# Fused filter, code and mixture-of-experts kernel: whole tiles counted in two parts, means and scales in the lists' entries

## Chip, cores and metric

The kernel runs on one core of one Trainium2 chip, in one launch. The metric is device time in microseconds: the median of the runs of a kernel, each the time of that one core. Three runs of the kernel before gave 1426.52 us at the median, 1426.07 to 1428.13.

## The reference

The input x is 16 x 1024 tokens of 512 numbers (16,384 tokens, fp32). For each token:

```python
xn = layernorm(x)                                   # no weights
x1 = ifft(fft(xn) * filt).real                      # filt from the first 1024 numbers of xn
bits = sigmoid(x1 @ W_el + b_el) > 0.5              # 24 bits
corrected = golay_correct(bits)                     # syndrome of 12, up to 3 flips
s = x1 + corrected @ W_le + b_le
probs = softmax(xn @ router_w.T)                    # 8 experts
top 2 of probs; weights = top2 / (sum + 1e-6)
ffn = sum over the two: (xn @ expert_w[e] + prob[e]) * weight[e]
out = x + s * silu(ffn)
```

So each token needs two products of 512 x 512 with the weights of its own two experts.

## The kernel before

Tokens are worked on 128 at a time, a *tile*; there are 128 tiles. The kernel has two passes.

**Pass 1** (`pass_1`, a loop over token tiles g) runs over the tokens in their order. Per tile: sums on VectorE (`total`) and squares on ScalarE (`spread`) for mean and scale; folding of the input into its even and odd halves (`fold`, one part of it, `mm`, on GpSimd); four transposes and the filter matmuls on TensorE (`transpose`, `filt`), whose output also holds the 24 code values and the 8 router values; evacuation on ScalarE, and a store of the filtered part to the DRAM tensor `yd` per four tiles (`store`, SyncE's queue). Per eight tiles the code is corrected (`code`: bits, two turns by TensorE, syndrome, correction). Per *round* of tiles the router runs (`route`): some fifty small VectorE steps that find the two largest experts, their weights and the position of each token in a list, and then one scatter DMA per tile (`scatter`, GpSimd's queue) that writes the token's number to that position in the DRAM tensor `lists`. There are 28 lists, one for each pair of experts. Rounds have 16 tiles up to tile 96, then 8, and at last 4 and 4. The steps of a round wait in the Python list `routes`; `push(n)` emits up to n of them per tile (4, then 7, then three times 12) and stops at a `None`, and `throw` emits one or two scatters per tile. All emission is by hand (`manual_schedule`): each engine executes its instructions in the order in which the program emits them, and a wait holds all that follows on that engine. `put_records` stores 32 numbers per token (weights, bias, mean in column 10, scale in column 11, code bits) to the first columns of `yd`.

After the last tile the last round runs alone, then the counts: `whole_a`, `whole_b` and `whole_c` work out how many full tiles of 128 each pair's list holds, fetch the list rows of the 101 *whole tiles* by one indirect DMA (`tt`, L887) and transpose them, which gives `toks` (the token of each partition for each whole tile) and `woff` (the two experts of each whole tile). `rest_a`, `rest_b`, `rest_c` work out where the remaining tokens of each list lie (`row_r`).

**Pass 2** runs over 189 tiles in an order fixed in advance: 101 *whole* tiles (one pair of experts for all 128 tokens, two products of four 512-wide steps each, L1186), 61 *items* (rest tokens gathered for one expert, one product, result stored to `ed`), and 27 *rests* (rest tokens again, which gather their two results from `ed` as `part0` and `part1`). The order is 10 wholes, then 61 items with 18 wholes among them, 4 wholes, then 27 rests with 69 wholes among them, each rest ahead of two or three wholes. The loop's turn n emits, in this order, work for tiles ahead and behind:

```python
each(n + AHEAD_K, fetch_tok)      # 9 ahead: list entries of items and rests
each(n + AHEAD_X, fetch_x)        # 6 ahead: x, and the row of yd
each(n + AHEAD_P, fetch_parts)    # 4 ahead: rests only
each(n + AHEAD_N, normalize)      # 3 ahead: DVE
each(n + AHEAD_N + 1, triple)     # 4 ahead: copy of the code bits, DVE
each(n, spread_out); each(n - 1, combine)          # DVE
put(tiles[n - 4])                 # BEHIND = 3: out <- xg, indirect DMA
work_on(tiles[n], beside)         # products; beside: turn(n+2), mend(n+1), turn_code(n+3)
```

All gathers and `put` are indirect DMAs on GpSimd's queue. `gather` is the helper at L1108; the write-out to `out` is L1266. `combine` adds into the buffer of x (`xg`) and `put` writes it out, so this buffer is held from `fetch_x` until its write-out has landed. Buffers per name: `xg` 14, `yg` (the row of `yd`) 11, `xn2` 4, `res` 3. The pools of pass 1 are closed before pass 2; the framework makes an instruction wait for the last user of a buffer that it takes over. Address work of items and rests (`side`) runs one step per turn on VectorE.

Of the kernel before, what the change touches and what calls it, by code (L numbers as in the profile page):

```python
# [22 lines left out]
BITS = 24  # L23
# [9 lines left out]
def kernel(  # L33
# [31 lines left out]

    nc = tc.nc
# [20 lines left out]
    NITEM = 2 * NREST + NE - 1  # L87

# [4 lines left out]
    lists = dram.tile([NPAIR * N, 1], I32, name="lists")  # L93
# [8 lines left out]

    p1 = ExitStack()

    front = p1.enter_context(tc.tile_pool(name="front", bufs=2))
    xin = p1.enter_context(tc.tile_pool(name="xin", bufs=5))
    work = p1.enter_context(tc.tile_pool(name="work", bufs=2))
    sp = p1.enter_context(tc.tile_pool(name="sp", bufs=1))
    small = p1.enter_context(tc.tile_pool(name="small", bufs=3))
    mid = p1.enter_context(tc.tile_pool(name="mid", bufs=1))  # L110
    p1c = p1.enter_context(tc.tile_pool(name="p1c", bufs=1))
    cs = p1c.tile([P, X + Q], F32, name="cs")
    cd = p1c.tile([P, X + Q], F32, name="cd")
    cm = p1c.tile([P, 2, X + H], F32, name="cm")
# [10 lines left out]
    NR = 6 * NPAIR + 2 * NPAIR  # L125
    ord_sb = p1c.tile([NPAIR, orders.shape[1]], F32, name="ord_sb")
    upto_o = ord_sb[:, 0:NPAIR]
    uptoid_o = ord_sb[:, 0 : 2 * NPAIR]
    at = 2 * NPAIR
# [48 lines left out]
    zero = w_sb[:, NE - 4, 0, :].bitcast(I32)  # L178
# [55 lines left out]

    def clear_lists():
        nc.gpsimd.memset(zero, 0)
        nl = NPAIR * N // P // 512
        nc.gpsimd.dma_start(
            out=lists.rearrange("(p a n) o -> p a (n o)", p=P, a=nl),
            in_=zero.unsqueeze(1).to_broadcast([P, nl, 512]),  # L240
        )
# [170 lines left out]

    PAIRED = NT - 4 * GT
    rounds = [(t, 2 * GT) for t in range(0, PAIRED, 2 * GT)]
    rounds += [(t, GT) for t in range(PAIRED, NT - GT, GT)]
    rounds += [(NT - GT, TPT), (NT - TPT, TPT)]
# [3 lines left out]
    ps_g = p1.enter_context(tc.tile_pool(name="ps_g", bufs=2, space=PSUM))  # L420
# [3 lines left out]
    recs = [p1c.tile([P, 2 * GT, META], F32, name=f"rec{i}") for i in range(3)]  # L424
# [13 lines left out]
    for s in range(NG):  # L438
        groups[s].rec = recs[(s // 2) % 3][:, (s % 2) * GT : (s % 2 + 1) * GT, :]
# [28 lines left out]
    def spread(g: int):  # L468

        k, j = groups[g // GT], g % GT  # L470
        no = small.tile([P, E], BF16, name="no", bufs=2)
        nc.scalar.activation(  # L472
            no, xts[g // TPT][:, g % TPT, :], AF.Square, bias=k.sum[:, j : j + 1],
            scale=-float(E), accum_out=k.sq2[:, j : j + 1],
        )
# [81 lines left out]
    def take_ex(b: int, first: int = 0, past: int = TPT):  # L557

        s, a = b * TPT // GT, b * TPT % GT
        k = groups[s]  # L560
        if s * GT < PAIRED and s % 2:
            k.ex = groups[s - 1].wide[:, GT:]
        elif a + first == 0:
            k.wide = front.tile([P, 2 * GT, X], F32, name="ex")
            k.ex = k.wide[:, 0:GT]
        y = ybs[b][:, first:past]
        nc.vector.tensor_add(k.ex[:, a + first : a + past], y[:, :, 0, 0:X], y[:, :, 1, 0:X])
# [55 lines left out]
    def put_records(t, n):  # L623
        r = recs[(t // (2 * GT)) % 3]
# [6 lines left out]
    def route(n: int):  # L631
# [17 lines left out]
        def begin():  # L649
            s, j = t0 // GT, t0 % GT  # L650
            st.ex = (groups[s].wide if t0 < PAIRED else groups[s].ex)[:, j : j + S]
            st.rec = recs[(t0 // (2 * GT)) % 3][:, t0 % (2 * GT) : t0 % (2 * GT) + S, :]
            st.mx = st.m1 = new("mx", [P, S])
            v.tensor_reduce(st.mx, st.ex[:, :, L:X], AX.X, ALU.max)

# [36 lines left out]
        final = n + 1 == len(rounds)  # L692
        ops = [begin] if final else [begin, shift]
        ops += largest(lambda: st.ex[:, :, L:X], "hot1")
        if final:
            ops += [shift]
# [90 lines left out]
        def scatter(j):  # L787
# [4 lines left out]
                in_=tok[:, t0 + j : t0 + j + 1],  # L792
# [40 lines left out]
        if final:  # L833
            return ops + [None, rank, quads] + ranks + [None] + chances + weights
        ops += [quads, None, rank] + chances + weights
        ops += [lambda: put_records(t0, S)] if t0 + GT < NT else []
        return ops + ranks
# [9 lines left out]
    toks = bt.tile([P, NPURE], I32, name="toks")  # L847
    woff = bt.tile([1, 2 * P], I32, name="woff")
# [12 lines left out]
    def whole_a():  # L861

        pc = ps_g.tile([P, 512], F32, name="pg")[0:NPAIR, 0:P]
        nc.tensor.matmul(pc, cum, ones_b, start=True, stop=True)
        md.full = mid.tile([NPAIR, P], F32, name="full")
        floors(md.full, pc, 0.5 - P / 2)
        md.cnt = mid.tile([NPAIR, P], F32, name="cntk")
        nc.vector.tensor_copy(md.cnt, pc)

    def whole_b():  # L870

        po = ps_g.tile([P, 512], F32, name="pg")[:, 0 : 2 * NPAIR]
        nc.tensor.matmul(po, md.full, uptoid_o, start=True, stop=True)
        f = mid.tile([P, NPAIR], F32, name="upto_f")
        nc.vector.tensor_copy(f, po[:, 0:NPAIR])
        step = mid.tile([P, NPAIR], F32, name="step")
        nc.vector.tensor_scalar(step, po[:, NPAIR:], -1.0, float(NT), ALU.mult, ALU.add)
        scr = mid.tile([P, NPAIR], F32, name="scr")
        at = mid.tile([P, 3], F32, name="at3")
        for i, st_ in enumerate((step, steplo_r, stephi_r)):  # L880
            nc.vector.scalar_tensor_tensor(
                scr, f, tf, st_, ALU.is_le, ALU.mult, accum_out=at[:, i : i + 1]
            )
        idx = mid.tile([P, 1], I32, name="idx")
        nc.vector.tensor_add(idx, at[:, 0:1], tf)
        md.tt = mid.tile([P, P], I32, name="tt")
        nc.gpsimd.indirect_dma_start(  # L887
            out=md.tt[0:NPURE, :],
            out_offset=None,
            in_=lists.rearrange("(r c) o -> r (c o)", c=P),  # L890
            in_offset=bass.IndirectOffsetOnAxis(ap=idx[0:NPURE, :], axis=0),
            bounds_check=NPAIR * N // P - 1,
            oob_is_err=False,
        )
        pi = ps_g.tile([P, 512], F32, name="pg")[0:1, 0 : 2 * P]
        for h in range(2):
            nc.tensor.matmul(
                pi[:, h * P : (h + 1) * P], at[:, 1 + h : 2 + h], ident, start=True, stop=True
            )
        for h in range(2):  # L900
            nc.vector.tensor_scalar(
                woff[:, h * P : (h + 1) * P], pi[:, h * P : (h + 1) * P], float(h), None, ALU.add
            )

    def whole_c():

        tf_ = mid.tile([P, P], F32, name="ttf")
        nc.vector.tensor_copy(tf_[0:NPURE, :], md.tt[0:NPURE, :])
        pt = ps_g.tile([P, 512], F32, name="pg")[:, 0:NPURE]
        nc.tensor.transpose(pt, tf_[0:NPURE, :], ident[0:NPURE, 0:NPURE])  # L910
        nc.vector.tensor_copy(toks, pt)

    def rest_a():

        ph = ps_g.tile([P, 512], F32, name="pg")[0:NPAIR, 0:P]
        nc.tensor.matmul(ph, upto_o, md.full, start=True, stop=True)
        md.h = mid.tile([NPAIR, P], F32, name="h")
        nc.vector.tensor_scalar(md.h, ph, float(NPURE), None, ALU.min)

    def rest_b():  # L920

        pl = ps_g.tile([P, 512], F32, name="pg")[0:NE, 0:P]
        nc.tensor.matmul(pl, len_o[:, 0:NE], md.cnt, start=True, stop=False)
        nc.tensor.matmul(pl, len_o[:, NE:], md.h, start=False, stop=True)
        md.c = mid.tile([NE, P], F32, name="c")
        floors(md.c, pl, P / 2 - 0.5)

    def rest_c():
        pr = ps_g.tile([P, 512], F32, name="pg")[:, 0:NR]
# [4 lines left out]
        nc.vector.tensor_copy(row_r, pr)  # L934
# [4 lines left out]
    step_i = row_r[:, 4 * NPAIR + SEG :]  # L939
    GI = 8  # L940

    def item_adr(j: int, room):
# [6 lines left out]
            qf[:, j : j + n].unsqueeze(2).to_broadcast([P, n, SEG]),  # L949
# [5 lines left out]
        nc.vector.tensor_add(adr_i[:, j : j + n], jump, qf[:, j : j + n])  # L955

    def item_experts(room):
# [8 lines left out]
        with nc.allow_low_precision("whole numbers"):  # L966
            nc.vector.tensor_reduce(ioff[:, 0:NITEM], cmp, AX.X, ALU.add)

    def rest_adr(i: int, room, first, past):
# [14 lines left out]
        nc.vector.tensor_add(adr_r[:, i, first:past], jump, q)  # L984

    def pass_1():
        now, routes, scales = [], [], []

        def push(n):

            done = 0
            while routes and done < n:
                op = routes.pop(0)
                if op is None:
                    return
                op()
                done += 1

        def throw(n):
            for _ in range(min(n, len(scatters))):  # L1000
                scatters.pop(0)()
# [15 lines left out]
        for g in range(-2, NT):  # L1017
            if (g + AHEAD_L) % TPT == 0 and 4 <= (g + AHEAD_L) // TPT < NB:
                xts[(g + AHEAD_L) // TPT] = load_block((g + AHEAD_L) // TPT)
            if g == 2:  # L1020
                clear_lists()
# [4 lines left out]
            if g == NT - 1:  # L1026
                take_ex(NB - 1, 0, TPT - 1)
# [16 lines left out]
            if g % GT == 1 and g > 1:  # L1044
                now = code(g // GT - 1)
            if g == NT - TPT:
                last = code(NG - 1)
            for n, (t, size) in enumerate(rounds):
                if g == t + size + 1:
                    routes += route(n)  # L1050
            if now:
                now.pop(0)()
            if g < PAIRED:
                push(4)
            elif g < NT - TPT:
                push(7)
            else:
                for _ in range(3):
                    push(12)
# [389 lines left out]
```

## Time and profile before

| what | us |
|---|---|
| median of three runs | 1426.52 |
| the profiled execution, device time | 1425.39 |
| its span, first to last instruction | 1423.6 |
| last filter matmul of pass 1 starts | 355.86 |
| first expert product of pass 2 starts | 397.76 |
| last product of pass 2 ends | 1414.2 |
| expert products (L1186) busy on TensorE | 942.1 |
| GpSimd busy (917 instructions, mostly indirect DMAs) | 926.1 |
| VectorE busy / ScalarE busy | 955.1 / 594.2 |

The profile is one execution. "Busy" counts instructions with work; gaps are put down to what ended them, in the form `[idle <-releaser]`. "issue" means that nothing the profile shows was waited for. PE is TensorE's matmul, PEld its weight load, DVE is VectorE, ACT ScalarE, POOL GpSimd, SP SyncE. A line of the timeline has the start in us, the length in us, the engine, the line of the kernel, the operation and its operands. The landing time of a DMA runs from the start of the issuing instruction.

### The profile page before, as it was taken

Reading aid. Unit: us, or ns where it says so; the run is one execution under the profiler, and the core shown is the slowest. Engines: PE = TensorE matmul, PEld = TensorE weight load, DVE = VectorE, ACT = ScalarE, POOL = GpSimd, SP = SyncE. Lnnn points to the kernel's source line nnn. Section 1 sums busy time; section 2 is a strip of 40 time slices with the busy share of each in tenths; the row PEclk is TensorE's granted clock in tenths of the full one; section 3 lists DMA queues with packets and bytes.
Section 4 is the critical chain, followed back from the end, with each engine's and each line's share of the span. In section 5 each row is a group of like instructions: output and inputs, shape, how many; then the busy total and the mean of one; then the engine's idle time right before and its main releaser. Section 6 shows DMA issues by size and latency. Waiting matters only on the chain.

```text
span 1423.6 us, 18981 instructions
## 1 busy us (share of the span) xinstructions
PE 1349.6 (95%) x5189; PEld 760.1 (53%) x5189; DVE 955.1 (67%) x2703; ACT 594.2 (42%) x1297; POOL 926.1 (65%) x917
## 2 busy tenths in 40 slices
PE   2999999988399999999999999999999999999997
PEld 2888888766144444444444444444444444444443
DVE  7798888898368733333323336777877778777785
ACT  4889899875022222222222232333333333333332
POOL 1347777786464676676666567777777777777731
PEclk9999999999589999999999999999999999999999
DMA  5898777743141343444444465555555555555521
GB/s 202 320 322 279 225 230 238 215 130 98 55 136 63 129 147 108 137 138 114 122 145 127 123 190 171 174 169 171 165 175 172 173 173 166 173 173 160 182 95 45
DMA packets 119317, 232.39 MB, mean 163 GB/s; under 512 B 35925, under 2 KB 70565, under 8 KB 115118
## 3 DMA queue, kind: packets, MB, share of 16 engines
q0 software_dynamic: 49472, 135.96, 32.2%
q1 hardware_dynamic: 68638, 94.43, 20.4%
q8 instruction: 46, 0.75, 0.2%
q10 hardware_dynamic: 1104, 0.78, 0.2%
q14 instruction: 57, 0.47, 0.2%
HBM read 144.00 MB, written 87.10 MB: 162 GB/s over the span
## 4 chain that ended last, share of the span: by engine, by line
PE 65%; issue 5%; POOL 2%; DMA 1%; DVE 1%; POOLq 0%; ACT 0%; DVEq 0%
PE pe L1186 58%; PE pt L1159 5%; PE pe L1218 2%; POOL out L1266 1%; DMA tt<-lists,idx 0%; PE pc L1207 0%; POOL xg L1108 0%; POOL yg L1108 0%; DMA yg<-yd,toks 0%; DVE acc L1234 0%; DMA xg<-in_x,toks 0%; DVE yg L1223 0%; POOL part L1108 0%; POOL lists L789 0%; DVE mix L1260 0%
## 5 line engine op out<-in xcount | busy, mean ns | idle before, releaser
L1186 PE MATMUL pe<-w_sb,xt 128*128 x2104 | 942.1, 596 | 0.4 <-ACT ct L1211 0.4
L1186 PEld LDWEIGHTS pe<-w_sb,xt 128*128 128x128 f32 x2104 | 387.2, 190 | 425.4 <-issue 413.7
L1235 ACT ACTIVATE acc<-acc,yg 128x512 f32<-128x512 f32 x128 | 92.5, 722 | 407.5 <-DVE acc L1234 407.5
L1234 DVE SCALAR_TENSOR_TENSOR acc<-pe,yg,acc 128x512 f32<-128x512 f32 x101 | 75.7, 749 | 217.3 <-PE pe L1186 217.3
L1266 POOL DMA_INDIRECT out<-xg,toks x101 | 109.7, 1086 | 84.4 <-DVE xg L1261 63.7
L1161 ACT COPY xt<-pt 128x512 f32<-128x512 f32 x162 | 93.8, 579 | 163.7 <-PE pt L1159 112.5
L512 POOL TENSOR_TENSOR mm<-xt 128x256 f32<-128x256 f32 x128 | 98.6, 771 | 96.2 <-PE pt L519 70.9
L539 PE MATMUL py<-cm,pmt 128*128 128x288 f32 x512 | 158.9, 434 | 0.0
L789 POOL DMA_INDIRECT lists<-tok,dst x128 | 130.7, 1021 | 41.3 <-issue 20.7
L1108 POOL DMA_INDIRECT xg<-in_x,toks x101 | 108.9, 1078 | 39.7 <-issue 33.2
L1108 POOL DMA_INDIRECT yg<-yd,toks x101 | 106.3, 1053 | 33.3 <-issue 23.8
L1231 ACT ACTIVATE acc<-pe,yg 128x512 f32<-128x512 f32 x101 | 68.9, 682 | 139.9 <-PE pe L1186 119.4
L1159 PEld LDWEIGHTS pt<-ident,xn 128*128 128x128 f32 x648 | 81.5, 142 | 85.0 <-issue 84.1
L1223 DVE TENSOR_TENSOR yg<-pe,yg 128x512 f32<-128x512 f32 x128 | 87.3, 682 | 58.8 <-PE pe L1218 58.8
L1108 POOL DMA_INDIRECT rec<-yd,at x61 | 63.2, 1036 | 83.5 <-DVE at L1131 71.0
L542 ACT ACTIVATE yb<-py,rec 128x576 f32<-128x576 f32 x128 | 94.9, 741 | 39.9 <-PE py L539 39.2
L1108 POOL DMA_INDIRECT xg<-in_x,tok x88 | 93.8, 1066 | 26.9 <-issue 26.9
L1159 PE MATMUL pt<-ident,xn 128*128 128x128 f32 x648 | 98.2, 275 | 0.2
L539 PEld LDWEIGHTS py<-cm,pmt 128*128 128x128 f32 x512 | 89.1, 194 | 13.9
L472 ACT ACTIVATE no<-xt,sum 128x512 bf16<-128x512 f32 x128 | 91.0, 711 | 2.0 <-DVE pp L452 2.0
L1261 DVE TENSOR_TENSOR xg<-mix,xg 128x512 f32<-128x512 f32 x128 | 88.6, 692 | 4.4
L1260 DVE TENSOR_TENSOR mix<-mix,acc 128x512 f32<-128x512 f32 x128 | 87.9, 687 | 4.5 <-ACT acc L1235 4.5
(255 smaller groups left out, 1817.1 us busy)
## 6 DMA issues: line engine op xcount, KB each, us to landing
xt<-in_x SPq DMA_DIRECT2D x32, 1024.0 KB, 9.3
yd<-yb SPq DMA_DIRECT2D x64, 512.0 KB, 4.7
ed<-res SPq DMA_DIRECT2D x61, 256.0 KB, 3.5
w_sb<-in_expert_w SPq DMA_DIRECT2D x8, 1024.0 KB
yd<-rec SPq DMA_DIRECT2D x32, 64.0 KB, 2.9
lists<-tok,dst POOLq DMA_INDIRECT x128, 4.8
lists<-w_sb POOLq DMA_DIRECT2D x1, 1792.0 KB, 8.8
xg<-in_x,toks POOLq DMA_INDIRECT x101, 3.5
```

What stands on the lines that cost most here:

```text
L472: nc.scalar.activation(no, xts[g // TPT][:, g % TPT, :], AF.Square, bias=k.sum[:, j : j + 1], scale=-float(E), accum_out=k.sq2[:, j : j + 1],)
L512: nc.gpsimd.tensor_tensor(m, xr[:, 0:H], xr[:, H:E], ALU.subtract)
L539: nc.tensor.matmul(py[:, 1, 0 : X + H], pmt[:, 2 + c, :], cm[:, c, :], start=(c == 0), stop=(c == 1))
L542: nc.scalar.activation(y_room(g), py[:, :, 0:WY], AF.Copy, scale=k.rec[:, j, 11:12])
L789: dma = nc.gpsimd.indirect_dma_start(out=lists, out_offset=bass.IndirectOffsetOnAxis(ap=st.dst[:, j : j + 1], axis=0), in_=tok[:, t0 + j : ...
L1108: nc.gpsimd.indirect_dma_start(out=dst, out_offset=None, in_=src, in_offset=bass.IndirectOffsetOnAxis(ap=idx, axis=0), bounds_check=limit - 1,
L1159: nc.tensor.transpose(pt[:, c * P : (c + 1) * P], k.xn[:, c * P : (c + 1) * P], ident)
L1161: nc.scalar.copy(k.xt.rearrange("p c t -> p (c t)"), pt)
L1186: nc.tensor.matmul(pe.unsqueeze(1), k.xt[:, c, :], w_sb[:, bass.ds(e, 1), c, :], start=(c == 0), stop=(c == KC - 1),)
L1235: nc.scalar.activation(k.acc, k.acc, AF.Silu, bias=k.rec[:, 9:10])
L1261: nc.vector.tensor_add(k.x, k.mix, k.x)
L1266: dma = nc.gpsimd.indirect_dma_start(out=of, out_offset=bass.IndirectOffsetOnAxis(ap=k.tok, axis=0), in_=k.x, in_offset=None, bounds_check ...
```

## The change

- **Lists hold entries of three words**: mean, scale, token. The scatter sends columns 10 to 12 of the record (`ENTRY`), and `begin` of each round copies the tokens to column 12. The code bits move up in the record (`BITS` 24 to 26). Lists are no longer cleared at the start; `item_ends` caps item positions at the end of each expert's section (`qc`) instead.
- **Counting in two parts.** `whole_a`, `whole_b`, `whole_c` and `rest_a` become `whole_ops(part)`, a list of small steps in the queue `aside`. Part 0 takes 30 whole tiles from the lists as they stand after tile 80 and runs inside pass 1; its fetch waits until the scatters known at that point have been emitted. Part 1 takes the other 71 and runs in pass 2. `toks`, `woff` and the new `stats` (means and scales, turned along with the tokens) exist once per part.
- **All rounds have 16 tiles**, `push` takes 4 steps and `throw` one scatter per tile throughout pass 1. The last round, the code of the last eight tiles, part 1 of the counts, `rest_b` to `rest_e` and the address work run in `beside` of pass 2's turns, up to ten steps and three scatters a turn.
- **Order of pass 2**: 28 wholes, 61 items, 5 wholes, 27 rests with 68 wholes among them.
- **Gathers**: an item's or rest's list entry brings mean and scale, so items no longer gather a record (`rec`, with its VectorE step `at`). The row of `yd` is gathered by a step of its own, `fetch_y`, 4 tiles ahead instead of 6.
- **Buffers**: `xg` 11 (14), `yg` 7 (11), `xn2` 3 (4), `res` 2 (3), `recs` 4 (3). The pools `small`, `mid`, `p1c` and the PSUM pool `ps_g` stay open through pass 2; `turn_code` takes its PSUM from `ps_g`. `xin` is now the first pool of pass 1.

The diff, cut to its core:

```diff
+ENTRY = slice(10, 13)
-BITS = 24
+BITS = 26
...
+    SOON = 80
+    PARTS_OF = (30, NPURE - 30)
...
-    lists = dram.tile([NPAIR * N, 1], I32, name="lists")
+    lists = dram.tile([NPAIR * N, 3], I32, name="lists")
...
+    RT = 2 * GT
+    rounds = [(t, RT) for t in range(0, NT, RT)]
...
             v.tensor_reduce(st.mx, st.ex[:, :, L:X], AX.X, ALU.max)
+            v.tensor_copy(st.rec.bitcast(I32)[:, :, 12], tok[:, t0 : t0 + S])
...
-                in_=tok[:, t0 + j : t0 + j + 1],
+                in_=st.rec.bitcast(I32)[:, j, ENTRY],
...
+    def whole_ops(part: int):
...
+        def lengths():
+            nonlocal due
+            due = thrown[0] + len(scatters)
+            k.pc = ps_g.tile([P, 512], F32, name="pg")[0:NPAIR, 0:P]
+            nc.tensor.matmul(k.pc, cum, ones_b, start=True, stop=True)
...
+        def fetch():
+            if thrown[0] < due:
+                return False
+            nc.vector.tensor_copy(woff[part], k.pi)
+            k.tt = mid.tile([P, P, 3], I32, name="tt")
+            nc.gpsimd.indirect_dma_start(
+                out=k.tt[0:n].rearrange("t c o -> t (c o)"),
...
+        aside.extend([lengths, None, full, None, rows_, None, where, upto, None, experts])
+        aside.extend([bounded, None, fetch, None, None, apart, None, turned, None, kept])
...
-            if g == 2:
-                clear_lists()
+            if g == 20:
+
+                put_records(NT - RT, RT, recs[3])
...
                 if g == t + size + 1:
-                    routes += route(n)
+                    routes.extend(route(n))
+                    if t + size == SOON:
+                        routes.append(lambda: whole_ops(0))
...
+            push(routes, 4)
+            push(aside)
+            throw(1)
...
-    AHEAD_K, AHEAD_X, AHEAD_P, AHEAD_N, AHEAD_T = 9, 6, 4, 3, 2
+    AHEAD_K, AHEAD_X, AHEAD_P, AHEAD_Y, AHEAD_N, AHEAD_T = 9, 6, 4, 4, 3, 2
...
-    xgp = ctx.enter_context(tc.tile_pool(name="xgp", bufs=14))
+    xgp = ctx.enter_context(tc.tile_pool(name="xgp", bufs=11))
...
+    def fetch_y(k):
         if k.kind == "item":
...
-            row = w2.tile([P, E + META], F32, name="yg", bufs=11)
...
+            return
+        row = w2.tile([P, E + META], F32, name="yg", bufs=7)
+        gather(row, yd, k.tok, N)
...
-    LEAD, PAUSE, AMONG = 10, 4, 18
+    LEAD, PAUSE, AMONG = 28, 5, 0
...
+    now += code(NG - 1)
+    routes += route(len(rounds) - 1) + [lambda: whole_ops(1)] + [None] * 7
+    routes += [rest_b, None, rest_c, None, rest_d, None, rest_e, None]
...
                 each(n + AHEAD_N, turn_code)
+                if n < 0:
+                    return
+                if now:
+                    now.pop(0)()
+                push(routes, 10)
+                push(aside)
+                throw(3)
```

## Prediction

> **What bounds the kernel now.** I read the page's busy shares and slices first, then the seam between its two passes on TensorE, then that seam on GpSimd (POOL), then POOL late in pass 2.
>
> ```profile
> PE 1349.6 (95%) x5189; PEld 760.1 (53%) x5189; DVE 955.1 (67%) x2703; ACT 594.2 (42%) x1297; POOL 926.1 (65%) x917
> ...
> PE   2999999988399999999999999999999999999997
> ...
> POOL 1347777786464676676666567777777777777731
> PEclk9999999999589999999999999999999999999999
> ```
>
> TensorE is the bound, but for one hole in slices 8 to 10. The table by stretches measures it: TensorE has no gap in pass 2 and is mostly idle before.
>
> ```profile
> 348.00:392.00 44.00, 13.83 (x61) 9.03 (x61) 19.71 (x118) 3.88 (x9) 22.37 (x22) 0.55 0.17 47
> ...
> 398.00:1414.00 1016.00, 1016.00 (x2996) 489.63 (x2996) 629.69 (x1424) 308.18 (x602) 681.59 (x639) 1.00 0.48 146
> ```
>
> (Columns after the length: busy us of PE, PEld, DVE, ACT, POOL.) The hole's edges, and what POOL does in it:
>
> ```profile
> 355.86 2.27 PE L539 MATMUL py<-cm,pmt 128*128 128x288 f32 x4
> ...
> 397.76 5.06 PE L1186 MATMUL pe<-w_sb,xt 128*128 x8 [0.39 <-ACT ct L1211]
> ...
> 403.37 7.08 PE L1186 MATMUL pe<-w_sb,xt 128*128 x16
> ```
>
> ```profile
> 369.55 0.97 POOL L789 DMA_INDIRECT lists<-tok,dst  x1 [0.31 <-issue]
> 375.10 2.28 POOL L887 DMA_INDIRECT tt<-lists,idx  x1 [4.57 <-issue]
> 383.91 1.05 POOL L1108 DMA_INDIRECT xg<-in_x,toks  x1 [6.53 <-DVE toks L911]
> 387.67 1.00 POOL L1108 DMA_INDIRECT yg<-yd,toks  x1 [2.71 <-DVE row_r L934]
> ```
>
> The last filter matmul ends at 358.1; the first expert product starts at 397.8. Between them come scatters, their landing, the list fetch, and the first gathers. Last, POOL in the tail of pass 2, where whole tiles and rests alternate:
>
> ```profile
> 1023.60 1.09 POOL L1266 DMA_INDIRECT out<-xg,tok  x1 [0.30 <-DVE mix L1227]
> 1024.99 1.03 POOL L1108 DMA_INDIRECT xg<-in_x,tok  x1 [0.30 <-issue]
> 1026.33 1.01 POOL L1108 DMA_INDIRECT yg<-yd,tok  x1 [0.31 <-issue]
> 1027.65 1.03 POOL L1266 DMA_INDIRECT out<-xg,toks  x1 [0.30 <-issue]
> 1028.98 1.03 POOL L1108 DMA_INDIRECT tok<-lists,adr_r  x1 [0.30 <-issue]
> 1030.32 1.23 POOL L1108 DMA_INDIRECT xg<-in_x,toks  x1 [0.31 <-issue]
> ```
>
> It issues one indirect DMA after another. Its groups from 850 to 1250 us are 274 instructions, 295 us busy, 105 us idle; 274 gaps of 0.30 are 82 of these, so POOL really waits only some 22 us in 400. Busy share (74%) hides that it is **94% occupied**, one step behind TensorE. The page's landing times matter next:
>
> ```profile
> out<-xg,toks POOLq DMA_INDIRECT x101, 3.0
> ```
>
> **What the Trainium skill says.** "DMA: Bandwidth & Descriptors", section "Anatomy of one DMA — SWDGE (gpsimd) path": a semaphore wait is served on the issuing sequencer before dispatch, and each DMA has about 2.0 us of fixed cost, mostly the write receipt. The trace agrees: `out` lands 3.0 us after its start, 1.03 of them POOL's. "Perfetto Trace Analysis", section "Optimization Strategy": an equal bubble that repeats can mean that buffers ran out; before has none on TensorE. "TensorE: Matmul & The Clock Gate", section "What's actually happening": about 3.4 us idle halve the clock. The trace agrees: PEclk 5 in slice 10, and 5.06 us for eight products that later take 3.46.
>
> **The change, part by part.**
>
> *Pass 1.* Y evacuations on ScalarE stand at 39.98 (token tile 0), 264.60 (tile 96) and 358.16 (tile 127): 2.34 us a tile, then 3.02, when `push(7)` and rounds of 8 and 4 begin. Rounds of 16 at `push(4)` go on throughout, so I take 31 x 2.34: tile 127 at 337.1. The count behind tile 80 adds small matmuls, some 1.5 us of TensorE, and one fetch on POOL. That fetch stands behind the last scatter's landing (4.57 us of waiting in the trace) and takes 2.28; the next round's scatter, in the same step, may not write the lists before the fetch has landed (6.84 us from its start). Queued behind is `mm`, which the transposes need, at most two tiles (4.7 us) ahead. So TensorE loses 0 to 8 us; I take 5. Tile 127: 343.6. Clearing the lists (8.8 us of DMA near the start) goes: nothing, since TensorE stays at 100% over it. Entries of 12 bytes instead of 4 keep the instruction count and 128 elements; no row shows them: -5 to +5 us, value 0.
>
> *Start of pass 2.* Tokens, means and scales of 30 whole tiles are known; `xg` can be gathered early, but `yg` needs the last y store: 343.6 + 0.74 evacuation + 4.7 landing = 349.0. From the first `yg` to the first product took 397.76 - 387.67 = 10.1 us; the order of gathers is the same, so the product starts at 359.1: **38.7 us earlier**. The cold clock after the hole stays.
>
> *What moved into pass 2.* TensorE: code, rank and list matmuls of the hole sum to 10.0 us at the half clock, some 5.5 at full clock, plus 1.5 for a rank of 16 tiles: **+7**. VectorE: a whole tile costs 5.0 us (ten rows' means, from xn 0.54 to acc 0.75) of a 7.63 us turn; a round of 16 sums to 13.3 us over six turns, 2.2 each: 7.2, it fits. ScalarE: at most two more function-table switches; "ScalarE: Activation LUTs", section "What ACT_TABLE_LOAD costs", gives 1.28 us, no run here shows it; ScalarE is 30% busy: 0, without that cover 2.6. POOL: round 6 begins at step 113 and reaches its scatters ten steps of `push(4)` later, so 5 of its 16 go out in pass 1; 11 and round 7's 16 are left, three a turn; with xg, yg and out 6 x 1.34 = 8.0 us against 7.63; and scatters wait for `dst`, which VectorE makes in the same turn, with all gathers queued behind. The last records' store on SP waits for the `yg` gathers before it, and later ones wait for it (2.9 us). Count matmuls sit right behind `cum` in one turn (2 to 3 us of TensorE), and code turns share two PSUM buffers with the counts (2 + 1.5). With 3 for POOL I take **+10**, range 3 to 20. Items lose 61 `rec` gathers and `at` steps on POOL and DVE: 0, TensorE has no gap there now. The order (28 wholes, items, 5 wholes, rests) has the same products.
>
> So the seam gives -38.7 + 7 + 10 = **-22** (-32 to -5).
>
> *Buffers.* This decides. At the top of turn n a buffer for the x of tile n+6 is taken. Tiles n-4 to n+5 hold ten: tile n-4 is written out only at that turn's end. Of 14 buffers four are free, the oldest for four turns. **Of 11 one is free: that of tile n-5, whose `out` was POOL's last instruction of the turn before.** So each `xg` must wait until that `out` has landed. POOL is in order: `yg`, the parts and the next `out` are queued behind, VectorE's code copy and sum wait for that `yg` (its lead shrinks from 6 turns to 4, with 7 buffers for 11), and TensorE waits for both. Price: `xg` starts 3.0 + 0.25 after `out` starts, not 1.38 (1.08 + 0.30): **+1.87 us a turn**; with a `tok` gather between, 3.25 - 2.76 = +0.49. Items hold no buffer after normalizing, and early turns have slack (3 x 1.38 + 1.87 = 6.0 against 7.63). In the tail a cycle is one rest and 68/27 = 2.52 wholes. TensorE: 2.52 x 7.63 + 0.66 = 19.9. POOL: 6 + 7.56 = 13.56 gathers x 1.38 = 18.7, plus 2.52 x 1.87 + 0.49 = 5.2: **23.9 us**. POOL becomes the bound by 4.0 us a cycle. Turns 94 to 182 are 89, or 25.3 cycles: 101 us, less one turn of lead (8): **+93**. Ends: landing 2.7 and 1.34 an instruction give 22.5 a cycle, +51 in all; a release 0.9 later, as the list fetch saw after its scatter, gives 27.2, +177.
>
> **Sum.** -22 + 93 = +71 on the span of 1423.6 (the profiled execution took 1425.4, the median is 1426.5): 1497 us.
>
> **Rivals.** *The seam alone* (faster): the `out` wait isn't there, or is covered. For it: before never waits there. Against: 94% occupancy leaves 1.2 us a cycle. It gives 1426 - 22 = 1404, or 1394 at best. *Break-even*: landing so quick that the tail costs just 22, which is 0.9 us a cycle, or 1.3 with the lead: an added wait of 0.9 us per `out` instead of 1.87; 1426. Slower begins beyond that. *Lockstep* (slower still): a release 0.9 us later, and holes over 3.4 us that halve TensorE's clock; 1426 - 5 + 177 = 1598. *The change doing nothing to the seam*, because yd's dependences hold the first gathers until the counts are done: 1426 + 93 = 1519 with the tail.
>
> **Chances.** POOL-bound tail 0.64 at about 1497, with lockstep 0.10 and unchanged seam 0.06 beside it: slower 0.80. Seam alone 0.17, break-even 0.03. The likeliest case's own range is 1440 (1426 - 32 + 51 is 1445, rounded down) to 1600. The range reaches down to 1412, to take in break-even and the dearer end of the seam alone. What can be told from no change is 0.2%, 2.9 us.
>
> **What would show it.** In the profile after: first product near 359; `xg` with some 2 us of idle time behind `out` from turn 94 on, not 0.30; tail cycles of 24 us, not 19.9; TensorE with gaps in the last third only. I am wrong if `xg` follows `out` at 0.30, or if TensorE stays at 100% there.

## The result, and the profile after

After takes **1552.68 us** at the median of four runs (1550.52 to 1556.75), against 1426.3 for before on the same chip: a ratio of 1.0887 [1.0862, 1.0912], 8.9% slower. The profiled execution has a span of 1548.7 us (before: 1423.6). The forecast was 1497 us, in a range of 1412 to 1600.

The page of after, the lines that answer to those of before:

```profile
PE 1388.9 (90%) x5194; PEld 763.5 (49%) x5194; DVE 945.5 (61%) x2549; ACT 593.3 (38%) x1293; POOL 874.2 (56%) x855
...
PE   3999999987889999999999998878897878888886
...
POOL 1357777767474456754432556555665556665551
```

The hole at the seam is filled but for a dent: its lowest slice has 7 where before had 3. In its place stands a comb, mostly of 7s and 8s, from the 25th slice to the end, where before had 9s up to its last slice. POOL is *less* busy there than before (5s and 6s for 7s), although it does the same work per tile. The table by stretches gives both places in numbers (columns after the length: busy us of PE, PEld, DVE, ACT, POOL, then TensorE's clock, the DMA share and GB/s):

```profile
348.00:392.00 44.00, 34.41 (x107) 16.68 (x108) 23.38 (x67) 14.11 (x26) 30.07 (x29) 0.79 0.43 123
...
870.00:1490.00 620.00, 527.85 (x1436) 239.96 (x1434) 387.35 (x847) 160.99 (x327) 369.65 (x331) 0.96 0.43 132
```

The seam won: 34.41 us of TensorE work where before had 13.83 in the same 44 us. The tail lost: 92 of 620 us without a matmul, and no engine is near its limit by its busy time. The timeline of POOL in the tail tells why:

```profile
1099.09 1.04 POOL L1318 DMA_INDIRECT out<-xg,toks  x1 [0.30 <-issue]
1102.25 1.12 POOL L1145 DMA_INDIRECT xg<-in_x,toks  x1 [2.13 <-DMA out<-xg,toks]
...
1114.22 1.04 POOL L1318 DMA_INDIRECT out<-xg,entry  x1 [0.30 <-issue]
...
1117.49 1.09 POOL L1145 DMA_INDIRECT xg<-in_x,entry  x1 [0.90 <-DMA out<-xg,entry]
```

Each gather of x stands behind the write-out ahead of it until that has landed: it starts 3.16 us after the write-out's start (1102.25 - 1099.09). In before, the gather right behind a write-out started after 1.3 to 1.4. With a list gather between, the start comes at the same distance (1117.49 - 1114.22 = 3.27), and the visible wait is 0.90. The waits of POOL from 870 to 1490 us (total us, times, longest), then those of TensorE over the whole run:

```profile
POOL xg L1145 <- DMA out<-xg,toks: 145.0, 61, 3.5
...
POOL xg L1145 <- DMA out<-xg,entry: 25.3, 24, 2.3
```

```profile
PE pe L1236 <- DVE yg L1273: 61.5, 47, 4.5
```

TensorE's longest list entry names VectorE's sum into `yg`. But VectorE is only 62% busy in the tail (387.35 of 620): the page has its copy of the code bits, which stands ahead of that sum, waiting for the row gather:

```profile
L1251 DVE COPY b<-yg 128x96 bf16<-128x96 bf16 x128 | 25.6, 200 | 244.1 <-DMA yg<-yd,toks 138.7
```

And the row gather is queued behind the x gather on POOL. The named releaser is the last link; the first is the landing.

### The profile page after: what moved, and what is told of

Same layout as the page of the kernel before. It is cut to its first block, busy times and chain, and to the rows that moved or that the text cites. A ratio compares the mean times of both kernels' runs of the same rounds, so it can differ in the third digit from the quotient of the medians.

```text
span 1548.7 us, 18669 instructions
## 1 busy us (share of the span) xinstructions
PE 1388.9 (90%) x5194; PEld 763.5 (49%) x5194; DVE 945.5 (61%) x2549; ACT 593.3 (38%) x1293; POOL 874.2 (56%) x855
## 4 chain that ended last, share of the span: by engine, by line
PE 33%; issue 25%; POOL 16%; DMA 3%; DVE 2%; POOLq 1%; ACT 0%; SPq 0%; DVEq 0%; ACTq 0%
PE pe L1236 27%; POOL out L1318 6%; POOL yg L1145 5%; PE pt L1204 2%; POOL xg L1145 2%; POOL part L1145 2%; DMA out<-xg,entry 1%; POOL entry L1145 1%; PE py L535 1%; DMA yg<-yd,toks 1%; DMA out<-xg,toks 1%; POOLq L1145 0%; PE pt L515 0%; PE pe L1268 0%; DMA yd<-yb 0%
## 5 line engine op out<-in xcount | busy, mean ns | idle before, releaser
L1236 PE MATMUL pe<-w_sb,xt 128*128 x2104 | 978.2, 613 | 62.3 <-DVE yg L1273 61.5
L1236 PEld LDWEIGHTS pe<-w_sb,xt 128*128 128x128 f32 x2104 | 394.8, 196 | 516.3 <-issue 465.7
L1251 DVE COPY b<-yg 128x96 bf16<-128x96 bf16 x128 | 25.6, 200 | 244.1 <-DMA yg<-yd,toks 138.7
L783 POOL DMA_INDIRECT lists<-rec,dst x128 | 131.6, 1028 | 56.2 <-issue 22.0
L1145 POOL DMA_INDIRECT xg<-in_x,entry x88 | 90.8, 1032 | 107.3 <-DVE xn L1197 49.8
L1145 POOL DMA_INDIRECT yg<-yd,toks x101 | 123.1, 1219 | 45.0 <-issue 29.2
L1197 DVE TENSOR_SCALAR xn<-xg,entry 128x512 f32<-128x512 f32 x61 | 34.4, 564 | 175.1 <-PE pt L1204 172.0
```

The source lines that it names most:

```text
L783: dma = nc.gpsimd.indirect_dma_start(out=lists, out_offset=bass.IndirectOffsetOnAxis(ap=st.dst[:, j : j + 1], axis=0), in_=st.rec.bitcast( ...
L1145: nc.gpsimd.indirect_dma_start(out=dst, out_offset=None, in_=src, in_offset=bass.IndirectOffsetOnAxis(ap=idx, axis=0), bounds_check=limit - 1,
L1236: nc.tensor.matmul(pe.unsqueeze(1), k.xt[:, c, :], w_sb[:, bass.ds(e, 1), c, :], start=(c == 0), stop=(c == KC - 1),)
```

## Experiments

Eight of the twelve ran on two chips on which the kernel before took 1472.9 and 1468.7 us at the median, with waits in the traces that no instruction of the kernel explains; so each ratio is to before on the same chip, and absolute times of different chips are not compared. The last four ran on a chip where before took 1429.96. Beside the ratio stands the **tail cycle**: from the first `part` gather of the first rest to that of the last, divided by 26. Before has (1354.59 - 845.68) / 26 = 19.57 us, after (1485.19 - 837.25) / 26 = 24.92. The expectations of experiments 1 to 4 give times in us as for the chip of the result (before at 1426); on the chip where they ran, only the ratios and the cycles can be held against them.

Theory: 11 buffers for x leave no spare one, so each gather waits for the landing of the write-out just issued. Rivals: the shorter lead of the row gathers (4 turns for 6, 7 buffers for 11), the number of buffers as such, and the work inserted at the seam.

**1. One buffer more** (after_xg12).

```diff
-    xgp = ctx.enter_context(tc.tile_pool(name="xgp", bufs=11))
+    xgp = ctx.enter_context(tc.tile_pool(name="xgp", bufs=12))
```

> The kernel after the change with 12 buffers of xg instead of 11, nothing else. Buffer theory (each gather of x waits for the write-out issued just before it): one buffer to spare puts a whole turn of GpSimd work, at least 4 us, between a write-out and the gather that reuses its buffer, and a write-out lands in 3.1 us; so the tail falls back to about 19.6 us a cycle and the whole to 1426 - 14 = 1412 us, between 1405 and 1420. Rival, late row gathers (fetch_y 4 turns ahead with 7 buffers): the tail stays at 24 us or more a cycle, 1530 us or more. Rival, both share the loss: 1450 to 1500.

Measured: 0.9967 [0.9943, 0.9990], tail cycle 20.09 us; POOL no longer waits for `out`. One buffer takes away the whole loss. On this chip a gain of 0.3% is left instead of the 1% expected.

**2. One turn less ahead** (after_x5): 11 buffers, but x gathered five turns ahead.

```diff
-    AHEAD_K, AHEAD_X, AHEAD_P, AHEAD_Y, AHEAD_N, AHEAD_T = 9, 6, 4, 4, 3, 2
+    AHEAD_K, AHEAD_X, AHEAD_P, AHEAD_Y, AHEAD_N, AHEAD_T = 9, 5, 4, 4, 3, 2
```

> The kernel after the change with AHEAD_X 5 instead of 6: x is gathered a turn later, so that with the same 11 buffers one is spare. Buffer theory: as with 12 buffers, about 1412 us (1405 to 1425). Rival, that gathers come too late for VectorE: later gathers make it no better, 1550 us or more.

Measured: 0.9945 [0.9920, 0.9971], tail cycle 20.12. *Less* prefetch repairs the kernel as well as a buffer more does. It isn't the number of buffers, but the one spare.

**3. The loss in the kernel before** (before_xg11).

```diff
-    xgp = ctx.enter_context(tc.tile_pool(name="xgp", bufs=14))
+    xgp = ctx.enter_context(tc.tile_pool(name="xgp", bufs=11))
```

> The kernel before with 11 buffers of xg instead of 14, nothing else. Buffer theory: its tail goes from 19.6 to about 24.9 us a cycle, over some 25 cycles 130 us, and nothing is lost among items, which give their buffers back early: 1426 + 130 = 1556 us (1530 to 1580). Rival, that the loss comes from late row gathers, the order or the list entries: below 1440 us.

Measured: 1.0596 [1.0528, 1.0663], tail cycle 25.09 (24.9 expected; the time expected is a ratio of about 1.09). The timeline of its POOL has the same picture as after's:

```profile
1107.78 1.03 POOL L1266 DMA_INDIRECT out<-xg,toks  x1 [0.31 <-issue]
1110.97 1.03 POOL L1108 DMA_INDIRECT xg<-in_x,toks  x1 [2.17 <-DMA out<-xg,toks]
```

**4. The row gathers alone** (before_y4): before, with the row of `yd` gathered by a step of its own, 4 turns ahead, in 7 buffers.

```diff
+    def fetch_y(k):
+        if k.kind == "item":
+            return
+        row = w2.tile([P, E + META], F32, name="yg", bufs=7)
...
+            each(n + 4, fetch_y)
```

> The kernel before with the gather of the row of yd as a step of its own, 4 turns ahead and with 7 buffers instead of 6 ahead with 11, as in the change; xg keeps 14 buffers. Buffer theory: the gathers still come before their readers, 1426 us, at most 1435. Rival, late row gathers: most of the 126 us is here, 1500 us or more.

Measured: 1.0074 [1.0051, 1.0097], tail cycle 20.67. A loss (at most 1435 of 1426, or 1.006, was expected), but an eighth of that of experiment 3. This rival isn't the cause of the loss.

**5 to 7. How many buffers are enough, and another way to one** (after_xg13, after_behind2, before_xg12): after with 13; after with 11 and `BEHIND = 2` for 3, so that a tile is written out one turn earlier; before with 12 for 14.

```diff
-    xgp = ctx.enter_context(tc.tile_pool(name="xgp", bufs=11))    # after_xg13
+    xgp = ctx.enter_context(tc.tile_pool(name="xgp", bufs=13))
...
-    BEHIND = 3                                                    # after_behind2
+    BEHIND = 2
...
-    xgp = ctx.enter_context(tc.tile_pool(name="xgp", bufs=14))    # before_xg12
+    xgp = ctx.enter_context(tc.tile_pool(name="xgp", bufs=12))
```

> After with 13 x buffers instead of 11: two spare ones. Theory (a gather must wait only where the freed buffer's write-out was the instruction just before; one spare removes that): tail cycle as with 12 buffers, within 0.2 us, ratio to before 0.990 to 0.998. Rival (the write-outs' landing still costs something with one spare): a tail cycle shorter by 0.3 us or more, some 8 us in all.

> After with 11 buffers, but each tile is written out two turns behind its products instead of three: the same spare buffer won at the other end of its life. Theory: no gather waits for a write-out that was just issued, tail cycle near 20.1 to 20.6 us, ratio to before 0.990 to 1.003 (the write-out may wait for its vector sum now). Rival (the number of buffers itself, or the shorter lead of the row gathers, makes the loss): ratio over 1.05.

> Before with 12 x buffers instead of 14: the threshold from the other side. Theory (one spare buffer is enough): ratio 0.998 to 1.003. Rival (the loss grows with each buffer taken, 11 buffers cost 6%, so 12 cost some 4%): 1.03 or more.

Measured: 0.9973 [0.9951, 0.9995], cycle 20.18; 1.0033 [1.0009, 1.0057], cycle 20.62; 1.0049 [1.0024, 1.0075], cycle 20.49. One spare is enough (12 and 13 are the same in after), it can be won at either end of a buffer's life, and the step lies between 11 and 12, not in a slope. After_behind2 and before with 12 lose 0.3 and 0.5%, both just over what was expected; whether that is theirs or that chip's, I haven't separated.

**8. Moving three steps at the seam** (after_mend): after with 13 buffers; the counts of part 1 start a turn after the `cum` they read, the cut of the second list a turn after `where`, and the last round's scatters a turn after `dst`.

```diff
-        aside.extend([lengths, None, full, None, rows_, None, where, upto, None, experts])
+        aside.extend([None] * part + [lengths, None, full, None, rows_, None, where])
+        aside.extend([None] * part + [upto, None, experts])
...
-        ranks = [None, place, where]
+        ranks = [None, place, where] + [None] * (n + 1 == len(rounds))
```

> After with 13 x buffers, the counting matmul one turn behind the cum it reads, the second list's cut matmul one turn behind the vector work beside it, and the last round's scatters one turn behind dst. Theory (the seam's gain of 36.5 us is eaten in part by TensorE waiting inside turns for vector results made in the same turn: starts 3.1, cum 2.4, and POOL 16.6 for dst): 3 to 8 us under after_xg13, a ratio to before of 0.983 to 0.988, and no POOL wait over 5 us at the scatters. Rival (the lead's loss is the work itself and the half clock, not these waits): within 1.5 us of after_xg13.

Measured: 0.9985 [0.9965, 1.0006], not distinguishable from after_xg13, and above the 0.983 to 0.988 expected. By the medians alone (1463.05 and 1466.19) it is 3.1 us faster. In the trace, TensorE's waits for `starts` and `cum` (4.5 and 2.4 in after_xg13) are gone. They are in every version of after without the moves, and in neither of the two with them. POOL's wait at the scatters fell from 20.8 to 11.4 us, not under 5. What the moves are worth in time stays undecided on this chip: stray waits of TensorE in one place (up to 7.4 us here, 9.9 in after_xg13) are larger than the effect. Experiment 12, on the other chip, has these moves together with other edits.

**9 to 12. The parts on one chip** (before_same, after_same, before_order, after_best). Before_same and after_same are the two kernels unedited. Before_order has after's order of tiles and nothing else. After_best has the three moves of after_mend, 11 x buffers taken 5 turns ahead, and 9 row buffers gathered 5 turns ahead.

```diff
-    LEAD, PAUSE, AMONG = 10, 4, 18    # before_order
+    LEAD, PAUSE, AMONG = 28, 5, 0
...
-    AHEAD_K, AHEAD_X, AHEAD_P, AHEAD_Y, AHEAD_N, AHEAD_T = 9, 6, 4, 4, 3, 2    # after_best
+    AHEAD_K, AHEAD_X, AHEAD_P, AHEAD_Y, AHEAD_N, AHEAD_T = 9, 5, 4, 5, 3, 2
...
-        row = w2.tile([P, E + META], F32, name="yg", bufs=7)
+        row = w2.tile([P, E + META], F32, name="yg", bufs=9)
```

> The kernel before, unedited, for a trace from the chip on which the other experiments run. Theory (the gain of the seam is there, but waits that no instruction of the kernel explains, spread over all of pass 2 on this chip, blur it): first product near 400, the first part gather of the tail 36 us less 23 us, some 14 us, later in relation to it than in after, tail cycle 19.6 to 20.4 us. Rival (the row gathers' shorter lead eats the seam's gain): a tail cycle 0.4 us or more under that of after_xg12.

> After, unedited, on the chip of the experiments: the loss that the repairs are to be measured against. Theory (a POOL-bound tail hides other engines' stray waits, which before cannot hide): tail cycle 24.9 to 25.2 us as on the other chip, ratio to before 1.055 to 1.085, somewhat under 1.089.

> Before with the order of tiles of after alone: 28 wholes, the items, 5 wholes, then the rests among 68 wholes, instead of 10 wholes, the items among 18, 4, and the rests among 69. Theory (the products are the same and TensorE has no gap among either): ratio 0.998 to 1.003. Rival (items without wholes among them press on the stores, or the tail gets denser for POOL): 1.005 or more.

> After_mend's three moved steps, with 11 x buffers taken five turns ahead instead of six (a spare one), and the freed memory given to the row gathers: 9 buffers, five turns ahead instead of 4. Theory (spare x buffer, no in-turn waits at the seam, row gathers with more lead): the fastest of all, ratio to before 0.985 to 0.993, tail cycle 20.0 us or less. Rival (what is left of the loss is the inserted work and the half clock, and row gathers' lead does nothing): as after_mend, 0.996 to 1.000.

Measured: before_same one run, 1427.03, first product at 398.85, tail cycle 19.57; after_same 1.0891 [1.0870, 1.0912], cycle 24.88; before_order 1.0005 [0.9993, 1.0017], cycle 19.20; after_best **0.9839 [0.9820, 0.9858]**, 1407.73 against 1429.96, cycle 19.24. The version with the spare buffer and the mended seam beats both kernels. After_same lost slightly more than expected. The expectation took it that a chip with stray waits hides part of the loss, as the 1.06 of experiment 3 suggests; this chip turned out to have none of these waits, and the loss is that of the result. Before_xg11 wasn't run here, so the explanation is likely but not shown. Before_same's expectation misses too: the first `part` gather comes 6.6 us later than in after_same, not 14. Its rival's sign came true by the wording (19.57 is 0.5 under the 20.09 of after_xg12), but the two traces are of different chips, so it decides nothing.

Before_order, after_same and after_best have the same order of tiles, so three lines of TensorE's timeline cut each at the same places: the first expert product, the first whole after the items (x16), and the last products (x24). Before_order:

```profile
399.30 5.12 PE L1186 MATMUL pe<-w_sb,xt 128*128 x8 [0.39 <-ACT ct L1211]
...
854.98 7.08 PE L1186 MATMUL pe<-w_sb,xt 128*128 x16
...
1405.43 10.46 PE L1186 MATMUL pe<-w_sb,xt 128*128 x24
```

After_same:

```profile
362.32 6.00 PE L1236 MATMUL pe<-w_sb,xt 128*128 x8 [0.39 <-ACT ct L1261]
...
840.89 7.08 PE L1236 MATMUL pe<-w_sb,xt 128*128 x16
...
1528.29 10.46 PE L1236 MATMUL pe<-w_sb,xt 128*128 x24
```

After_best:

```profile
361.26 6.51 PE L1237 MATMUL pe<-w_sb,xt 128*128 x8 [0.38 <-ACT ct L1262]
...
831.84 7.08 PE L1237 MATMUL pe<-w_sb,xt 128*128 x16
...
1382.29 10.46 PE L1237 MATMUL pe<-w_sb,xt 128*128 x24
```

| us | before_order | after_same | after_best |
|---|---|---|---|
| start to first product | 399.30 | 362.32 (-37.0) | 361.26 (-38.0) |
| first product to end of items | 455.68 | 478.57 (+22.9) | 470.58 (+14.9) |
| tail, to the last products | 550.45 | 687.40 (+137.0) | 550.45 (0.0) |
| rest of the span | 19.87 | 22.81 (+2.9) | 22.81 (+2.9) |
| span | 1425.3 | 1551.1 (+125.8) | 1405.1 (-20.2) |

The tail of after_best is that of before_order to a hundredth: with a spare x buffer and the two more row buffers, TensorE alone sets it. In its POOL timeline the gather of x follows the write-out at once:

```profile
1103.25 1.29 POOL L1319 DMA_INDIRECT out<-xg,toks  x1 [0.73 <-DVE xg L1314]
1104.84 1.03 POOL L1146 DMA_INDIRECT xg<-in_x,toks  x1 [0.31 <-issue]
```

Between after_same and after_best the stretch from the first product to the end of the items is 8.0 us shorter. Gone are the waits for `starts` (3.9) and `cum` (2.4) and, behind each of them, a turn of sixteen products at a lowered clock (8.83 us for 7.08, twice 1.75; below): 9.8 us. Against that, after_best's first eight products take 0.5 longer, and it waits 0.9 for another vector result (`more`): 8.4 in sum. The moved steps account for the two waits. What the other edits that after_best joins bring was not tried one by one.

## Why the prediction was right, and where its sizes were off

*The bound, and the buffers as what decides*: right. TensorE is the bound of before, and GpSimd in after's tail, by waiting and not by work. Experiments 1 to 3 show it from both sides: one spare buffer removes the loss in after, and taking the spare ones away from before makes it.

*Pass 1*: the last evacuation was predicted at 343.6; the last filter matmul ends at 343.37 (342.15 + 1.22) and its evacuation starts at 343.40. That it fits to 0.2 us is in part luck. The count behind tile 80 was to cost TensorE 5 us of waiting; the one gap there is 1.36 us (before 298.22, for `mm`). The rate of 2.34 us a tile, on the other hand, was too low: 39.98 is the evacuation of the second tile, the first starts at 36.89, which gives 2.37, and at tile 96 after was already 1.45 us behind before (266.05 for 264.60).

*First product near 359, 38.7 us earlier*: 361.24 in the profiled execution, 36.5 earlier; 37.0 in after_same. The first row gather started at 351.33, not 349.0, since the last store of `yd` landed later; from there to the product it took 9.9 us (10.1 predicted).

*What moved into pass 2, 7 + 10*: 22.9 in after_same. The inserted TensorE work is about 7 and the waits sum to 9.7 there (9.0 in the profiled execution), both as predicted; missed was the clock. The timeline of TensorE in the profiled execution, at the counts of part 1:

```profile
413.36 0.23 PE L865 MATMUL pg<-ones_b,cum 128*28 128x128 bf16 x1 [2.39 <-DVE cum L826]
413.51 8.83 PE L1236 MATMUL pe<-w_sb,xt 128*128 x16
```

The wait for `cum` that the prediction names cost 2.39, and then the sixteen products took 8.83 instead of 7.08. In after_same the same happened again behind the wait for `starts` (3.88, then 8.83 for the sixteen products from 444.67), so the clock cost 3.5 there. The first eight products took 6.0 (5.1 in before_order), 0.9 more. About 2 of the 22.9 I can't place. So the seam gave -14.1 instead of **-22**, within the -32 to -5 given. After_best, without the two waits, has -23.1.

*ScalarE, at most two more table switches*: the trace has six table loads for before's four: two more. "ScalarE: Activation LUTs", section "What ACT_TABLE_LOAD costs", gives 1.28 us for the load, and the prediction said that no run here shows it. That was wrong: the groups of ScalarE show it in before's trace and in after's, 1283 ns for each load. The section also counts about 1.38 us of draining to every switch; here none shows: one load starts at 376.80, right behind a cast that ends at 376.79, and the next instruction starts at 378.10. That they cost nothing stands: the added loads lie at 376.80 and 378.33, and from 370 to 390 us TensorE has no gap (20.00 of 20).

*VectorE fits, items at 0, order at 0*: the items' stretch has TensorE at 100% (200.00 of 200 us from 600 on, in after and after_best), and before_order gives 1.0005.

*The tail, +93*: 137.0. This is **the term that was mis-sized**, in three places: the cycle, the lead, and the last turns.

- The cycle on POOL was to be 23.9 and is 24.9. Per wait: 145.0 / 61 = 2.38 us, less the ordinary gap of 0.30 is 2.08 for the predicted 1.87; with a list gather between 25.3 / 24 - 0.30 = 0.75 for 0.49. At 2.45 and 0.96 of these a cycle (61 and 24 in 620 / 24.92 = 24.9 cycles) that is 5.8 for 5.2. The instructions with their gaps are (369.65 + 331 x 0.30) / 24.9 = 18.8 for 18.7, and some 0.2 are a few longer waits: of row gathers (up to 2.1, some of them for `acc`, the last reader of their buffer) and of one x gather (3.6, no releaser named). TensorE takes 19.7 a cycle in before_order between the turns of the first and the last `part` gather (512.5 us in 26 cycles), so POOL is over it by 5.2 instead of 4.0: 134 us in 26 cycles.
- "Less one turn of lead (8)" was too much. The first `part` gather waits until the last item's result has been stored, and everything on POOL stands behind it:

```profile
837.25 1.00 POOL L1145 DMA_INDIRECT part<-ed,adr_r  x1 [33.45 <-DMA ed<-res]
```

  POOL idles 33 us there. The turn of the loop in which this gather stands has its first product on TensorE at 840.94, so POOL goes into the tail 3.7 us ahead, half a turn; at the last `part` gather it is 0.6 us ahead. So some 3 us come off, not 8. (In before POOL starts 3.5 us ahead and is 14.7 ahead at the last: there the lead is *built up* in the tail.) In after_same the 26 cycles take TensorE 643.6 us for before_order's 512.5, 131.1 more.
- The last turns, behind the last `part` gather, take 5.8 us more, and make up the 137.0.

*The end*: 2.9 us lie behind the last instruction of the timeline, in after_same and after_best alike. What they are, the trace doesn't show.

In sum: -22 became -14.1, +93 became +137.0, 0 became +2.9; 8 + 44 + 3 is what lies between the forecast and the time.

*Two slips in the sums*, neither of which decides: 22.5 a cycle would make +58, not +51, so the likeliest case's lower end should have been some 7 us higher; and 22 us and the lead are 1.2 a cycle, not 1.3.

*The rivals*: "seam alone" (1404) is near what the change comes to with a spare buffer, the moved steps and more row buffers: after_best is 22.2 us under before on its chip. That this is the -22 of this rival to 0.2 us is luck, since the parts differ (-38.0, +14.9 and +2.9 on the span, for -38.7 and +17). Break-even fell, since the added wait is 2.08 and not 0.9. Lockstep fell as a mechanism, though the measured time is nearer to its 1598 than to 1497: the release comes 0.2 later than reckoned, not 0.9, and the mean clock in the tail is 0.96 (0.94 in after_same), lowered only in short stretches. The unchanged seam fell. Of "what would show it", the gather's wait (2.1 to 2.4 us) and the gaps in the last third came as written; "24 us" was 24.9.

## What to carry to other kernels

Count a pool's buffers from the instruction that frees one to the instruction that takes it, on the queue that does both. Where the two are neighbours, as here, each use pays the landing of a transfer, and one spare buffer, or one turn less of prefetch, removed it. A queue worked in order at 94% occupancy had no room for such a wait, whatever its busy share said. And work that fills a hole gives back part of the gain where, within the same turn, it waits for a result made in that turn: here two such waits and the slower turns behind them took up to 9.8 of some 37 us.

## What was not expected of the hardware

A gap of 2.39 us on TensorE (410.97 to 413.36) was followed by a stretch at a clock of 0.59 (414 to 418 us) and a turn 1.75 us longer; the same gap in after_same gave the same 8.83. "TensorE: Matmul & The Clock Gate", section "What's actually happening", speaks of about 3.4 us idle; here less was enough, though there were shorter gaps in the 11 us ahead, too. But the length of the gap doesn't decide alone: in the same trace the longer one before 442.38 (3.11 us, for `starts`) was followed by a clock of 1.00 and sixteen products in 7.13, while in after_same the gap there was 3.88 and they took 8.83. No run isolates what else counts. In the tail, gaps of up to 4.5 us left the mean clock at 0.96.

The scatters of 12-byte entries land after 5.3 us at the median of after's page, those of 4 bytes in before after 4.8, and the same 12 bytes in after_best after 3.2, so these medians don't follow the size of the entry.
